# Running the last projection's eight row tiles inside attention

## The chip, the cores and the metric

The kernel runs on one core of one Trainium2 chip. The metric is device time in microseconds (us), the median of several runs. In the profile PE is TensorE, DVE is VectorE, ACT is ScalarE, POOL is GpSimd and SP is SyncE, which here issues every DMA.

## The reference

1024 rows x of 512 numbers are layer-normed. Two branches start from the normed rows xn: attention, and a feed-forward network with quantised weights, whose output goes through a SiLU and gates attention's output.

```python
xn = layernorm(x)
q = rmsnorm(heads(xn @ Wq.T)) ; k = rmsnorm(heads(xn @ Wk.T)) ; v = heads(xn @ Wv.T)   # 32 query heads, 8 key heads, 128 wide
scores = q @ k.T / sqrt(128) + slope[head] * (key - query)                             # causal
s = softmax(scores) @ v ; s = rows(s) @ Wo.T
g = silu(ffn(xn))
out = x + s * g
```

## The kernel before

Float32 products are made of three float16 products each (`mm3`, L151 to L153: high x high, high x low, low x high), added up in PSUM. Almost all PE work in this part is on these three lines, and it is told apart by its tiles.

The feed-forward network runs first, and its gates go to a scratch tensor `gd`. Then come twelve **projections**, numbered k = 0 to 11: for each pair of key heads one `kv` projection and two `q` projections of four heads. So k = 9 is the last `kv`, and k = 10 and 11 are the queries of groups 6 and 7. A projection has eight **row tiles** of 128 rows (`Projection.tile`): twelve products of 128x512 with the normed rows `xth`/`xtl` as weights and the projection's split weights `wh`/`wl` moving, into one PSUM slot of the ring "m" (even rows) or "o" (odd rows). ACT reads the slot (a copy into `f`, L660, and squares for the norm, L662; for `kv` also the values). Both rings have two slots, and attention uses them too: "o" for probabilities times values, "m" for the output projection.

After four tiles the half is queued (`queue_half`): the norms are inverted (L687), by a Sqrt on ACT and Newton steps on POOL (L707 to L710) where `by_root` holds, which is k < 10, and else by an integer seed on DVE (L130, L131) and Newton steps alone. Each tile is then normalised on POOL (`normalize`, L716) and split into two halves on DVE (`halves`, L729 and L730). Most pairs are transposed by DMA and stored (L752, L757, L759). Projection 10's are stored as they are (L735) and transposed when loaded, and projection 11's stay in SBUF until `last_queries` transposes them (L974). `prepare` splits the weights of the next projection meanwhile, on ACT (L631) and DVE (L633), and squares those of the one after (L570).

**Attention** goes in steps. A step n is one query tile of 128 rows of one head; there are 256, in blocks of eight: a group g of four heads and a block qb of 256 queries, in the order of `FIRST_ORDER`, `ORDER` and `LAST_ORDER` (within group 4: queries 2, 3, 0, 1, steps 128 to 159). PE's order in a step is written out by hand: the scores of step n, then the products of step n - 9 with the values (`values`), with a part of the output projection ahead of the last of them. The others follow at lags: DVE adds the position term and finds the maximum (`biased`, L1041) one step later, ACT takes exponentials (L1047) in the same step, ACT makes the high half (L1066) three steps later and DVE the low half (L1074) four steps later; then SP transposes both by DMA (L1082, or L1077 for queries 0) into `pT`, which is a slot of the ring "pT" or "wide". The output projection's weights are loaded (L991), scaled on POOL (L994) and split on ACT (L1000) and POOL (L1001). Sums of the output projection over the groups are kept in `y` rows (L1147, L1149), which lie in `xth`/`xtl`, since the last tile is done by then.

The first eight steps are hosted by projections 10 and 11: `project_all` calls `early_tile` after each of their 16 row tiles, which advances attention by half a step. A branch on the keys' lengths stands just before projection 10; the profiled execution takes the side where far keys of the steep heads are skipped.

The clock that `finishing` uses counts one per row tile, then one per step. So `TILES + 24` is step 32: the last projection's halves are inverted at steps 32 and 44 (`LAST_ROOTS`), and its pairs split at steps 54, 86, 118, 150, 182, 229, 232 and 237 (`LAST_PAIRS`, rows 4, 5, 6, 7, 2, 3, 0, 1).

Of the kernel before, what the change touches and what calls it, by code (L numbers as in the profile page):

```python
# [53 lines left out]
VALUES_STEP = 24  # L54


LAST_ROOTS = {1: 24, 0: 36}
LAST_PAIRS = {4: 46, 5: 78, 6: 110, 7: 142, 2: 174, 3: 221, 0: 224, 1: 229}
LAST_QUERIES = {4: 217, 5: 219, 6: 225, 7: 227, 2: 233, 3: 235, 0: 241, 1: 243}

WO_SPLIT = 6
WO_SCALE = 8
WO_LOAD = 10

GATE_LOADS = [211, 219, 235, 251]
GATE_SUMS = [227, 235, 251, 259]
PF_BUFS = 5
P16_BUFS = 5
OH_BUFS = 8
# [40 lines left out]
def attention_gated_by_ffn_kernel(ctx, tc, x, gu_w, gu_z, gu_s, dn_w, dn_z, dn_s, wq, wkv, wo, qnw, knw, out):  # L110
# [440 lines left out]
    class Projection:  # L551
# [97 lines left out]

        def tile(self, t):  # L650
            n, half, r = self.n, t // HT, t % HT
            if r == 0:
                self.f[half] = rings["f"].take(F32, HT, n, HD)
                self.ss[half] = rings["ss"].take(F32, HT, n)
                self.jk = rings["jk"].take(BF16, NH, HD)
            ps = ps1("o" if t % 2 else "m")
            rows = slice(t * P, (t + 1) * P)
            for j in range(KT):
                mm3(ps, (xth[:, j, rows], xtl[:, j, rows]), (self.wh[:, j, :], self.wl[:, j, :]), j == 0, j == KT - 1)
            se.copy(self.f[half][:, r], ps[:, : n * HD].rearrange("p (g d) -> p g d", g=n))  # L660
            for i in range(n):
                se.activation(  # L662
                    self.jk[:, i],
                    ps[:, i * HD : (i + 1) * HD],
                    AF.Square,
                    scale=STEEPER[i] / Q_SCALE if self.kind == "q" else 1.0,
                    accum_out=self.ss[half][:, r, i : i + 1],
                )
            if self.kind == "kv":
                if t == 0:  # L670
                    self.v16 = rings["v16"].take(F16, 2, NT, 2, HD)
                v16 = self.v16[:, :, t]
                vp = ps[:, 256:512].rearrange("p (g d) -> p g d", g=2)
                se.copy(v16[:, :, 0, :], vp)
                defer(1, lambda: ve.tensor_tensor(v16[:, :, 1, :], vp, v16[:, :, 0, :], ALU.subtract))
                if t == NT - 1:
                    defer(3, self.store_values)
# [227 lines left out]
    def pieces(tag, cols):  # L905
        return [slot[:, c : c + cols] for slot in rings[tag].slots for c in range(0, slot.shape[1], cols)]

    wh_pieces = pieces("wh", QB // 2)
    rings["oh"], rings["ol"] = Ring(wh_pieces[:OH_BUFS]), Ring(wh_pieces[OH_BUFS:])
    rings["wor"] = Ring(pieces("wl", DM))  # L910
    free_pieces = pieces("v16", DM // 2) + pieces("sq", DM // 2)
    rings["woh"], rings["wol"] = Ring(free_pieces[:5]), Ring(free_pieces[5:])
    y_halves = [t.rearrange("p k s -> p (k s)").bitcast(F32) for t in (xth, xtl)]

    def y_rows(t):
        return y_halves[t // HT][:, t % HT * DM : (t % HT + 1) * DM]
# [1 line left out]
    def queue_half(p, half):  # L918

        last = p is projections[-1]  # L920

        def due(steps, i, f):
            if last and i is None:
                c = TILES + LAST_ROOTS[half]
            elif last:
                c = TILES + LAST_PAIRS[half * HT + i] - 4
            else:
                c = clock[0] + (i or 0)
            finishing.setdefault(c + steps, []).append(f)

        due(0, None, lambda: p.inverse(half))
        if p.by_root:
            due(1, None, lambda: p.root(half))
            due(2, None, lambda: p.newton(half, True))
        else:
            for i in range(3):
                due((i + 1) // 2, None, lambda i=i: p.newton(half, i == 0))
        later = int(p.by_root)
        for i in range(HT):
            t = half * HT + i  # L940
            due(4 + later, i, lambda t=t: p.halves(t))
            due(2 + later, i, lambda t=t: p.normalize(t))
# [125 lines left out]
    def split_lo(u, qt):  # L1068
        p, h16 = pf.pop((u, qt)), p16.pop((u, qt))
        nk, k0 = p.shape[1], lowest(u, qt)  # L1070
        if qt == 0:
            pT[u] = rings["wide" if u % 4 < 2 else "pT"].take(F16, NT, 2, QB)
        hi, lo, scale = h16[:, :, 0, :], h16[:, :, 1, :], rows16[u][3][:, qt : qt + 1]
        ve.scalar_tensor_tensor(lo, p, scale, hi, ALU.mult, ALU.subtract)  # L1074
        if u in p16:
            if qt == NQT - 1:
                sp.dma_start_transpose(  # L1077
                    pT[u][:, :NQT].rearrange("p t a (i q) -> p (t a i) q", i=NQT),
                    p16.pop(u).rearrange("p t a i k -> p (t a i k)"),
                )  # L1080
            return
        sp.dma_start_transpose(  # L1082
            pT[u][:, k0 : k0 + nk, :, qt * P : qt * P + P].rearrange("p t a q -> p (t a) q"), h16.rearrange("p t a k -> p (t a k)")
        )
# [40 lines left out]

    gates = {}

    def gate_load(qb):
        gx = rings["f"].take(F32, 2, NQT, DM)
        t0 = qb * NQT  # L1130
        sp.dma_start(gx[:, 0], gd[t0 : t0 + NQT].rearrange("t p c -> p t c"))
        sp.dma_start(gx[:, 1], x[t0 * P : (t0 + NQT) * P, :].rearrange("(t p) c -> p t c", p=P))
        gates[qb] = gx

    def gate_partial(qb, i):

# [41 lines left out]
                        n, taken = n + 1, 0  # L1178
        free = n + (taken > 0)
    near = [False]  # L1180
    TILES = NT * len(projections)

    def at(n):

# [18 lines left out]
    def step(n):  # L1203
# [25 lines left out]
        if n < nn + AV_LAG + 1:  # L1229
            for due in acc_at.get(n, ()):  # L1230
                accumulate(*due)
        finish_step()

        def project():
            for due in op_at.get(n, ()):
                out_proj(*due)

        if at(n - AV_LAG):
            values(*at(n - AV_LAG), project)
        else:  # L1240
            project()
        if done is not None and units[done][:2] == final:
# [5 lines left out]
            if hh == NH - 1:  # L1248
                for due in acc_at.get(nn + AV_LAG + 1, ()):
                    accumulate(*due, other=True)  # L1250
                for i in range(NQT):
                    accumulate(g, qb, i)
        if n in GATE_LOADS:
            gate_load(LAST_ORDER[GATE_LOADS.index(n)][0])
        for i in range(NQT):
            if n - i in GATE_SUMS:
                gate_partial(LAST_ORDER[GATE_SUMS.index(n - i)][0], i)
        for lead, act in ((WO_SPLIT, split_wo), (WO_SCALE, scale_wo), (WO_LOAD, load_wo)):
            for g, first in op_first.items():
                if n + lead - first in range(0, 2 * NH, 2):  # L1260
                    act(g, (n + lead - first) // 2)

    last_ps = None

    def project_all(k):
        p = projections[k]
        for t in range(NT):
# [6 lines left out]
                    projections[k + 2].squares(i)  # L1274
            if t == HT:
                p.undo()
                if k == len(projections) - 3:
                    load_keys(0)
                    for qb in blocks[0][1]:
                        load_queries(0, qb)  # L1280
                elif k == len(projections) - 2:
                    load_values(0)
            if (k, t) == (len(projections) - 3, HT + 1):
                wo_squares_sums()

            row = t if k < len(projections) - 1 else (t + HT) % NT
            p.tile(row)
            finish_step()
            if t % HT == HT - 1:
                queue_half(p, row // HT)  # L1290
            c = (k - len(projections) + 2) * NT + t
            if c >= 0:
                for due in q_at.get(c // 2, ()) if c % 2 == 0 else ():
                    load_queries(*due)
# [4 lines left out]

    def attention(only_near):  # L1300
        near[0] = only_near
        for k in range(len(projections) - 2, len(projections)):
            project_all(k)
        for n in range(NT, nn + AV_LAG + 1):
            step(n)
# [16 lines left out]
                c[:] = old  # L1322

    relative(0)
    for k in range(len(projections) - 2):
        project_all(k)
    flag = nc.values_load(bounded[0:1, 0:1], min_val=0, max_val=1, skip_runtime_bounds_check_because="a comparison's result is 0 or 1")
    was = frozen()
# [44 lines left out]
```

## Time and profile before

| what | value |
|---|---|
| median of 3 runs | 1019.59 us (1016.86 to 1020.25) |
| the profiled execution | 1020.44 us, span 1018.6 us, granted PE clock 0.989 |
| row tiles of projection 9 (first to last L660) | 402.4 to 420.6 us |
| row tiles of projections 10 and 11 | 423.1 to 467.0 us |
| exponentials of steps 8, 16, 24 (L1047) | 469.6, 485.3, 497.4 us |
| exponentials of steps 48, 80, 112, 144, 176, 208 (queries 0 of groups 1 to 6) | 542.9, 605.5, 673.1, 744.8, 813.0, 881.6 us |
| last 8 steps and the end | 981.6 to 1018.6 us |

Times inside the span are counted from its start. A busy PE in the profile is not PE at its peak, since the products' ends are modelled and overlap; the distance between the starts of products is the better measure.

### The profile page before, as it was taken

Reading aid. Unit: us, or ns where it says so; the run is one execution under the profiler, and the core shown is the slowest. Engines: PE = TensorE matmul, PEld = TensorE weight load, DVE = VectorE, ACT = ScalarE, POOL = GpSimd, SP = SyncE. Lnnn points to the kernel's source line nnn. Section 1 sums busy time; section 2 is a strip of 40 time slices with the busy share of each in tenths; the row PEclk is TensorE's granted clock in tenths of the full one; section 3 lists DMA queues with packets and bytes.
Section 4 is the critical chain, followed back from the end, with each engine's and each line's share of the span. In section 5 each row is a group of like instructions: output and inputs, shape, how many; then the busy total and the mean of one; then the engine's idle time right before and its main releaser. Section 6 shows DMA issues by size and latency. Waiting matters only on the chain. (4 is left out here: it accounts for less than half of the span.)

```text
span 1018.6 us, 17980 instructions
## 1 busy us (share of the span) xinstructions
PE 964.7 (95%) x5688; PEld 561.8 (55%) x5688; DVE 857.2 (84%) x1764; ACT 775.5 (76%) x2160; POOL 429.4 (42%) x424
## 2 busy tenths in 40 slices
PE   6899999999999999996998999999999999989995
PEld 4344477854444444444555666665676666656562
DVE  7888998728888878877898998987989989969985
ACT  5777745778878887787887987987879978858861
POOL 2588764216666555564235151051241421530722
PEclk9999999999999999999999999999999999999999
DMA  7132359535998999998898999997999999999994
GB/s 251 37 121 93 104 170 310 187 125 163 204 273 190 245 229 215 236 237 202 172 196 161 206 216 183 227 203 158 231 202 191 212 201 190 202 219 198 218 201 108
DMA packets 425063, 195.74 MB, mean 192 GB/s; under 512 B 371522, under 2 KB 382078, under 8 KB 424958
## 3 DMA queue, kind: packets, MB, share of 16 engines
q1 hardware_dynamic: 424958, 194.50, 85.5%
q8 instruction: 46, 0.75, 0.3%
q14 instruction: 59, 0.48, 0.1%
HBM read 76.27 MB, written 27.27 MB: 102 GB/s over the span
## 5 line engine op out<-in xcount | busy, mean ns | idle before, releaser
L1074 DVE SCALAR_TENSOR_TENSOR p<-pf,row,p 128x384 f16<-128x384 f32 (+7 forms) x256 | 208.8, 816 | 20.9 <-ACT p L1066 18.0
L1047 ACT ACTIVATE pf<-pf,row 128x384 f32<-128x384 f32 (+7 forms) x256 | 184.9, 723 | 41.6 <-DVE row L1041 37.3
L1041 DVE CUSTOM_DVE_ANT_0 pf<-s,trel,cs 128x384 f32<-128x384 f32 (+7 forms) x256 | 191.4, 748 | 19.8 <-PE s L153 19.7
L1066 ACT ACTIVATE p<-pf,row 128x384 f16<-128x384 f32 (+7 forms) x256 | 184.0, 719 | 6.3 <-DMA pT<-p 1.4
L151 PE MATMUL s<-kT,qT 128*128 128x512 f16 (+3 forms) x356 | 115.3, 324 | 11.8 <-DVE row L1041 11.5
L994 POOL TENSOR_SCALAR wl<-wl,rvs 128x512 f32<-128x512 f32 x32 | 53.7, 1677 | 149.0 <-DMA wl<-in_wo 130.0
L152 PE MATMUL s<-kT,qT 128*128 128x512 f16 (+3 forms) x356 | 115.4, 324 | 0.0
L153 PE MATMUL s<-kT,qT 128*128 128x512 f16 (+3 forms) x356 | 114.0, 325 | 0.0
L716 POOL TENSOR_TENSOR f<-f,inv 128x512 f32<-128x512 f32 (+1 forms) x96 | 102.1, 1084 | 1.4
L151 PE MATMUL m<-v,wh 128*128 128x512 f16 x248 | 95.0, 383 | 0.0
L153 PE MATMUL m<-v,wh 128*128 128x512 f16 x248 | 94.9, 383 | 0.0
L151 PE MATMUL o<-pT,vT 128*128 128x256 f16 (+1 forms) x302 | 79.6, 264 | 13.9 <-DMA pT<-p 13.7
L151 PEld LDWEIGHTS <-vT 128*128 128x128 f16 x594 | 58.9, 99 | 57.8 <-DMA pT<-p 15.1
L1110 ACT ACTIVATE wh<-o 128x256 f16<-128x256 f32 x128 | 47.7, 373 | 54.4 <-PE o L153 53.8
L152 PEld LDWEIGHTS <-vT 128*128 128x128 f16 x594 | 58.9, 99 | 41.4 <-issue 4.5
L152 PE MATMUL o<-pT,vT 128*128 128x256 f16 (+1 forms) x302 | 79.6, 264 | 0.0
L153 PE MATMUL o<-pT,vT 128*128 128x256 f16 (+1 forms) x302 | 79.3, 264 | 0.0
L151 PE MATMUL o<-wide,vT 128*128 128x256 f16 (+1 forms) x292 | 75.9, 260 | 3.1 <-DMA wide<-p 3.1
L152 PE MATMUL o<-wide,vT 128*128 128x256 f16 (+1 forms) x292 | 75.9, 260 | 0.0
L153 PE MATMUL o<-wide,vT 128*128 128x256 f16 (+1 forms) x292 | 75.7, 260 | 0.0
L151 PE MATMUL m<-wh,xth 128*128 128x512 f16 x192 | 72.8, 379 | 1.2 <-ACT h L869 1.2
L153 PE MATMUL m<-wh,xtl 128*128 128x512 f16 x192 | 72.8, 379 | 0.0
(200 smaller groups left out, 2531.4 us busy)
## 6 DMA issues: line engine op xcount, KB each, us to landing
qd<-tr SPq DMA_DIRECT2D x48, 256.0 KB, 3.3
qT<-qd SPq DMA_DIRECT2D x24, 512.0 KB, 4.4
wide<-in_wq SPq DMA_DIRECT2D x32, 256.0 KB, 3.7
wo_sq<-in_wo SPq DMA_DIRECT2D x8, 1024.0 KB, 7.8
wl<-in_wo SPq DMA_DIRECT2D x32, 256.0 KB, 3.6
gui<-in_gu_w SPq DMA_DIRECT2D x13, 512.0 KB, 3.7
wide<-in_wkv SPq DMA_DIRECT2D x16, 256.0 KB, 3.8
vd<-v SPq DMA_DIRECT2D x8, 512.0 KB, 4.7
```

The costliest lines, as they stand in the source:

```text
L151: te.matmul(ps, lhsT=lh, rhs=rh, start=first, stop=False)
L152: te.matmul(ps, lhsT=lh, rhs=rl, start=False, stop=False)
L153: te.matmul(ps, lhsT=ll, rhs=rh, start=False, stop=last)
L716: ge.tensor_tensor(f, f, ib, ALU.mult)
L994: ge.tensor_scalar(wor[g, i], wor[g, i], rvs[:, g : g + 1], None, ALU.mult)
L1041: ve.tensor_tensor_reduce(p, ps, trel[g][:, S - w :], cs[:, hh : hh + 1], 3e38, ALU.add, ALU.min, least[:, c])
L1047: se.activation(p, p, AF.Exp, bias=least[:, c], scale=-1.0, accum_out=total[:, c])
L1066: se.activation(p16[u, qt][:, :, 0, :], pf[u, qt], AF.Copy, scale=scale[:, qt : qt + 1])
L1074: ve.scalar_tensor_tensor(lo, p, scale, hi, ALU.mult, ALU.subtract)
L1110: se.activation(oh, av_ps[u], AF.Copy, scale=1.0 / P_SCALE)
```

## The change

Projection 11 is no longer hosted ahead of attention. Projections 9 and 10 host the first eight steps, and the branch stands before projection 9. Each of projection 11's eight row tiles is issued within a step of attention (`LAST_TILES`: step 50 row 4, 53 row 5, 84 row 6, 119 row 7, 150 row 2, 182 row 3, 212 row 0, 215 row 1), behind the step's scores and ahead of its products with the values.

Since projection 11's weights and the normed rows are needed until step 215, buffers are given out otherwise: heads and Wo use the other projection's half of `wh` and `wl` and the ring "tr"; `y` lies in two slots of "f"; gates are loaded into the other two and into `xth`/`xtl`, each in four DMAs of a quarter at steps of their own instead of two DMAs; the first two of every four units use "pT" and the others "wide", the reverse of before. The half norms of projection 11 are inverted at steps 121 and 216, and its pairs split at steps 125, 150, 156, 184, 220, 229, 232 and 237. `by_root` is as it was.

```diff
-LAST_ROOTS = {1: 24, 0: 36}
-LAST_PAIRS = {4: 46, 5: 78, 6: 110, 7: 142, 2: 174, 3: 221, 0: 224, 1: 229}
+LAST_TILES = {50: 4, 53: 5, 84: 6, 119: 7, 150: 2, 182: 3, 212: 0, 215: 1}
+LAST_ROOTS = {1: 121, 0: 216}
+LAST_PAIRS = {4: 125, 5: 150, 6: 156, 7: 184, 2: 220, 3: 229, 0: 232, 1: 237}
 LAST_QUERIES = {4: 217, 5: 219, 6: 225, 7: 227, 2: 233, 3: 235, 0: 241, 1: 243}
...
-GATE_LOADS = [211, 219, 235, 251]
-GATE_SUMS = [227, 235, 251, 259]
+GATE_LOADS = {2: [186, 188, 190, 205], 3: [217, 218, 220, 222], 1: [225, 226, 228, 230], 0: [242, 244, 246, 248]}
+GATE_SUMS = {2: 227, 3: 235, 1: 251, 0: 259}
...
-    wh_pieces = pieces("wh", QB // 2)
-    rings["oh"], rings["ol"] = Ring(wh_pieces[:OH_BUFS]), Ring(wh_pieces[OH_BUFS:])
-    rings["wor"] = Ring(pieces("wl", DM))
+    LAST = len(projections) - 1
+    own = LAST % 2
+    head_pieces = pieces("wh", QB // 2)[(1 - own) * 8 : (2 - own) * 8] + pieces("tr", QB // 2)[8:]
+    rings["oh"], rings["ol"] = Ring(head_pieces[:OH_BUFS]), Ring(head_pieces[OH_BUFS : 2 * OH_BUFS])
+    rings["wor"] = Ring(pieces("wl", DM)[(1 - own) * 2 : (2 - own) * 2] + rings["tr"].slots[:2])
...
-    y_halves = [t.rearrange("p k s -> p (k s)").bitcast(F32) for t in (xth, xtl)]
+    y_halves = rings["f"].slots[:2]
+    x_halves = [t.rearrange("p k s -> p (k s)").bitcast(F32) for t in (xth, xtl)]
...
         def due(steps, i, f):
-            if last and i is None:
-                c = TILES + LAST_ROOTS[half]
-            elif last:
-                c = TILES + LAST_PAIRS[half * HT + i] - 4
+            if last and i is not None:
+                c = step_clock(LAST_PAIRS[half * HT + i]) - 4
             else:
                 c = clock[0] + (i or 0)
...
-            pT[u] = rings["wide" if u % 4 < 2 else "pT"].take(F16, NT, 2, QB)
+            pT[u] = rings["pT" if u % 4 < 2 else "wide"].take(F16, NT, 2, QB)
...
-    def gate_load(qb):
-        gx = rings["f"].take(F32, 2, NQT, DM)
-        t0 = qb * NQT
-        sp.dma_start(gx[:, 0], gd[t0 : t0 + NQT].rearrange("t p c -> p t c"))
-        sp.dma_start(gx[:, 1], x[t0 * P : (t0 + NQT) * P, :].rearrange("(t p) c -> p t c", p=P))
-        gates[qb] = gx
+    def gate_load(qb, i):
+        if i == 0:
+            homes = rings["f"].slots[2], *x_halves, rings["f"].slots[3]
+            gates[qb] = homes[LAST_ORDER.index((qb,))].rearrange("p (a t c) -> p a t c", a=2, t=NQT)
+        t = qb * NQT + i // 2
+        sp.dma_start(gates[qb][:, i % 2, i // 2], x[t * P : (t + 1) * P, :] if i % 2 else gd[t])
...
+    HOSTS = range(LAST - 2, LAST)
+
+    def step_clock(n):
+        return NT * LAST + n - NT
...
         finish_step()
+        for half, due in LAST_ROOTS.items():
+            if n == due:
+                queue_half(projections[LAST], half)
...
+        if n in LAST_TILES:
+            last_tile(LAST_TILES[n])
         if at(n - AV_LAG):
             values(*at(n - AV_LAG), project)
...
-            row = t if k < len(projections) - 1 else (t + HT) % NT
-            p.tile(row)
+            p.tile(t)
...
-        for k in range(len(projections) - 2, len(projections)):
+        for k in HOSTS:
             project_all(k)
...
-    for k in range(len(projections) - 2):
+    for k in range(HOSTS[0]):
         project_all(k)
```

## The prediction

> **What bounds the kernel now.** I read the busy totals first, then busy time by stretches cut where projections and attention blocks begin, then TensorE's own timeline where it stands idle, then ScalarE and VectorE rows for what moves.
>
> ```profile
> PE 964.7 (95%) x5688; PEld 561.8 (55%) x5688; DVE 857.2 (84%) x1764; ACT 775.5 (76%) x2160; POOL 429.4 (42%) x424
> ```
>
> TensorE is busy almost throughout, but the average hides the places where it waits. One row tile costs what lies between the first products of two consecutive tiles:
>
> ```profile
> 304.24 0.38 PE L151 MATMUL m<-wh,xth 128*128 128x512 f16 x1
> ...
> 306.83 0.38 PE L151 MATMUL o<-wh,xth 128*128 128x512 f16 x1
> ```
>
> That is 2.59 us for twelve products (0.216 us apart; the 0.38 overlaps its neighbours). In the stretches below the columns are length, then busy us (and instructions) of PE, weight loads, DVE, ACT and POOL, then granted clock, DMA share and GB/s.
>
> ```profile
> 402.40:423.10 20.70, 20.70 (x98) 9.45 (x97) 18.27 (x39) 14.64 (x63) 12.70 (x18) 1.00 1.13 251
> 423.10:445.50 22.40, 22.40 (x112) 10.56 (x110) 18.43 (x55) 19.21 (x87) 11.70 (x23) 1.00 1.05 253
> 445.50:467.00 21.50, 20.41 (x100) 9.60 (x98) 16.26 (x33) 15.61 (x77) 12.12 (x18) 1.00 0.76 191
> 467.00:485.30 18.30, 11.43 (x78) 7.64 (x78) 11.40 (x37) 14.96 (x49) 7.69 (x6) 0.85 0.88 194
> 673.10:693.30 20.20, 18.17 (x136) 12.77 (x134) 13.49 (x37) 10.71 (x34) 7.14 (x8) 0.92 0.94 184
> 744.80:761.50 16.70, 16.40 (x134) 12.05 (x133) 13.52 (x37) 10.63 (x34) 7.08 (x8) 1.00 1.06 198
> 761.50:774.10 12.60, 12.60 (x81) 7.12 (x80) 12.04 (x34) 11.74 (x33) 1.49 (x1) 1.00 0.85 176
> 774.10:790.80 16.70, 16.70 (x119) 10.45 (x117) 16.49 (x35) 15.25 (x33) 1.58 (x1) 1.00 1.03 206
> 881.60:905.50 23.90, 18.39 (x136) 12.68 (x134) 13.40 (x35) 10.75 (x35) 9.09 (x10) 0.93 1.08 213
> ```
>
> Rows 1 to 3 are projections 9, 10 and 11: PE is full, so each lasts eight tiles plus the scores that it hosts. Row 4 is the start of attention (steps 8 to 15): PE idles 7 us and nothing else is full, so it is a chain of latencies. Rows 6 to 8 are three undisturbed blocks of eight steps (group 4 queries 0 and 1, group 5 queries 2): PE is full in all three, but DVE has 3.2 us free in the first, 0.6 in the second and 0.2 in the third. Rows 5 and 9 are two more blocks of queries 0 (groups 3 and 6), 3.5 and 7.2 us longer than row 6 for the same work. Why is on PE's timeline; the bracket is the idle time and its releaser:
>
> ```profile
> 543.91 0.27 PE L151 MATMUL s<-kT,qT 128*128 128x256 f16 x1 [2.54 <-DVE row L1041]
> 612.27 0.27 PE L151 MATMUL s<-kT,qT 128*128 128x256 f16 x1 [0.75 <-DVE row L1041]
> 686.90 0.28 PE L151 MATMUL o<-pT,vT 128*128 128x256 f16 x1 [2.03 <-DMA pT<-p]
> 756.82 0.28 PE L151 MATMUL o<-pT,vT 128*128 128x256 f16 x1 [0.30 <-DMA pT<-p]
> 825.46 0.27 PE L151 MATMUL o<-pT,vT 128*128 128x256 f16 x1 [0.71 <-DMA pT<-p]
> 890.94 0.28 PE L151 MATMUL o<-pT,vT 128*128 128x256 f16 x1 [1.81 <-DMA pT<-p]
> 899.07 0.28 PE L151 MATMUL o<-pT,vT 128*128 128x256 f16 x1 [3.70 <-DMA pT<-p]
> ```
>
> The first two are ahead of the scores of steps 50 and 84. The other five stand between a step's scores and its products with the values, waiting for transposed probabilities, at steps 119, 151, 183, 212 and 215 (a step's time is read off the exponential of the step before, L1047). The new tiles stand in the same place of steps 119, 212 and 215, and one step earlier at 150 and 182.
>
> **The change, part by part** (against the profiled execution, 1020.44 us, 0.85 above the median of the three runs).
>
> (1) Projection 11's eight tiles leave the front. The eight hosted half-steps move one projection earlier, so their scores cost PE the same; 8 x 2.59 = 20.7 us of full PE go: **-20.7**.
>
> (2) Projection 9 now hosts exponentials, but still takes its roots with Sqrt, as only projections 10 and 11 avoid it. In program order ACT gets four more table loads (to Sqrt and back, twice: two in projection 9, two in 10).
>
> ```profile
> 430.35 1.28 ACT L1047 ACT_TABLE_LOAD   x1
> 431.65 0.51 ACT L1047 ACTIVATE pf<-pf,row 128x256 f32<-128x256 f32 x1
> ```
>
> One load is 1.28 us, and the next activation starts 0.02 us behind it, so four are 5.1 us. Projection 9's ACT: 14.64 + 3 exponentials and 2 scalings of 0.5 to 0.6 (2.7) + three loads (3.8) = 21.1 of 22.3 us. Projection 10's: 19.21 less one load, three exponentials and two scalings (3.9), plus four of each at 0.62 (4.9) and two loads (2.6) = 22.8 of 22.6. DVE in projection 9: 18.27 + 2.7 = 21.0 of 22.3. ACT is on average just full. In the tiles with a load to Sqrt or back it needs 3.8 to 4.6 us (load 1.3, reads 1.1 to 1.5, one or two squarings or a split of 0.65 to 0.74, an exponential or a scaling) against PE's 2.8, while PE's two accumulators allow about 1.3 us of lag. Behind the delayed reads waits PE's tile after next. The lag adds up to some 4.5 us: 4.5 - 1.3 = **+3** (bounds 0 and +5).
>
> The Trainium skill (ScalarE: Activation LUTs, "What ACT_TABLE_LOAD costs") speaks against this part: it counts a drain of about 1.38 us beside each load, some 2.66 us a switch. The row above shows no such gap. By the page four switches are an estimated 10.6 us and part (2) would be about +8, the total about 1016 to 1017.
>
> (3) Steps 8 to 15 take over what projection 11's first tiles hid: four normalisings on POOL (1.04 each where undisturbed), four splits on DVE, half of the stores of the pairs, and transposes and stores of projection 9 that SP is late with. A split is 0.42 + 0.69 = 1.1 us undisturbed; these means include disturbed ones:
>
> ```profile
> L729 DVE CAST a<-f 128x512 f16<-128x512 f32 x64 | 31.0, 484 | 6.8 <-POOL f L716 3.4 <-DMA tr<-a 3.4
> L730 DVE TENSOR_TENSOR a<-f,a 128x512 f16<-128x512 f32 x64 | 51.5, 804 | 2.2
> ```
>
> DVE gets 4.4 us more on 11.40 of 18.3 and still fits. SP does not so easily: between 446 and 467 us it issues some 17 us of transposes (1.2 to 1.3 each) and copies (about 0.55), which must now fit into a projection 9 where SP is already nearly full, or spill here, where some 4 us are free. Four normalisings stand among the scalings of Wo on POOL, which wait for loads through the same SP queue; DVE waits behind them. I take **+4**, between 0 (the latencies hide it) and +8 (12 us spill into 4 free).
>
> (4) The tiles inside attention, 2.59 us each, less the wait that each fills and the slow clock behind it (row 5: 0.08 x 20.2 = 1.6 us lost; row 9: 0.07 x 23.9 = 1.7; around 544, 0.13 of 13.3 = 1.7):
> - Steps 50 and 53: 5.2 - 2.5 - 1.7 = +1.0. The wait is ahead of scores, so the tile doesn't fill it; but its chain runs through POOL's Newton steps and Wo work from 531 to 540, and the Newton steps now stand at steps 121 and 216. Without them the block before, which idles 2 us, should save 1 more: 0.
> - Step 84: 2.6 - 0.75 = +1.8. Step 119: 2.6 - 2.0 - 1.6 = -1.0. Step 150: 2.6 - 0.3 = +2.3. Step 182: 2.6 - 0.7 = +1.9. Steps 212 and 215: 5.2 - 1.8 - 3.7 - 1.7 = -2.0.
>
> Sum **+3.0**, bounds -2 (more small waits fill) and +20.7 (none fills). ACT reads each tile in about 1.5 us; these blocks leave ACT 6 us idle (row 6). PE's products with the values are queued behind each tile; their accumulator is freed by DVE during it in most steps, and at 182, 84 and 212 one step later, under 1 us.
>
> On the slow clock, the Trainium skill (TensorE: Matmul & The Clock Gate, "What's actually happening") asks for an idle window of about 3.4 us. Here waits of 2.03 and 2.54 us already were followed by the slow clock reckoned above. By the page's figure only the wait of 3.70 would bring a credit, and the estimate would be some 3.3 us (1.6 + 1.7) higher.
>
> (5) Splits of four pairs move from blocks of queries 0, where DVE has 3.2 us free, to steps 125, 156, 184 and 220, in blocks of queries 1 where DVE has 0.6. Each adds 1.1 us: 0.5 to 1.1 late, taken as 0.7 since queries 2 behind it have nothing to give: **+2.8** (bounds 0, +4.4).
>
> (6) Gates come in sixteen DMAs of 0.5 us on SP instead of eight, earlier, between other issues. At the end POOL waits 4.15 us for one gate load; that wait should go, but the end hangs on DVE and PE. **0** (bounds -2, +2). Other buffers (pT before wide, y in f) cost nothing: what they hold is dead by then, and the waits that guard them end earlier.
>
> Sum: -20.7 + 3 + 4 + 3.0 + 2.8 + 0 = -7.9; on 1020.44 that is 1012.5, and 0.85 less at the median: 1011.7, rounded to **1011**.
>
> **Rivals.**
> - *Better:* the front absorbs everything and the splits hide: -20.7 + 1 + 0 + 1 + 0 = -18.7, about 1001. For it: row 4 has idle time on every engine. Against it: ACT at 101%.
> - *The front is the bound:* parts (2), (3) and (5) at their upper ends, 5 + 8 + 4.4, and (4) at +3: -0.3, about 1019. For it: SP and ACT are full before and after.
> - *Slower, the waits only move:* transposed probabilities come from SP's queue behind DVE, and DVE waits for PE's scores. If a tile delays the scores of the next steps and so the later transposes as well, the wait returns a few steps on and PE pays all of 20.7: -20.7 + 3 + 4 + 20.7 + 2.8 = +9.8, about 1029. It makes the kernel slower once less than 6.7 of the forecast's fill of 17.7 us (20.7 - 3.0) is real. Against it: the values lag scores by nine steps, so the transpose awaited was issued from scores long before the tile, and DMA goes on during the tile.
>
> **How the numbers follow.** Forecast 0.58 (1004 to 1016), better 0.14, front-bound 0.12, waits move 0.16. A difference of 0.3% (3 us) is about what a measurement of this kernel can tell from none. Faster: 0.58 + 0.14 + 0.03 = 0.75; same: 0.07 + 0.01 = 0.08; slower: 0.02 + 0.15 = 0.17. The range 1001 to 1021 leaves out the slower rival and a little of the better one.
>
> **What would show it.** Right: attention's step 8 starts 16 to 20 us earlier; step 16 about 14; the waits for pT ahead of products with the values at steps 119, 212 and 215 are gone or under 0.5 us, and the clock there is 1.00; blocks (4, 0) and (5, 0) are about 2 us longer; blocks (g, 1) with a split about 0.7 longer; ACT shows four table loads amid the projections, and L660 there waits less for PE. Wrong: PE idle in projections 9 and 10 above 5 us, steps 8 to 15 above 24 us, or a wait for pT in the steps just after each tile.

## The result and the profile after

The changed kernel takes 1028.37 us (median of 10 runs, 1026.27 to 1032.14) against 1019.95 for the kernel before on the same chip (10 runs, 1016.86 to 1026.79): a ratio of 1.0079, 95% interval 1.0057 to 1.0100. It is slower, where the forecast had 1011. The profiled execution took 1032.14 us (span 1030.3), 3.8 above the median.

The busy totals say little: the same work, spread over 11.7 us more.

```profile
PE 967.7 (94%) x5688; PEld 563.4 (55%) x5688; DVE 862.5 (84%) x1764; ACT 781.1 (76%) x2164; POOL 426.5 (41%) x424
```

Busy time by stretches of the changed kernel (columns as before: length, then busy PE, weight loads, DVE, ACT, POOL, then granted clock, DMA share, GB/s):

```profile
402.40:423.10 20.70, 19.33 (x96) 8.98 (x94) 17.05 (x42) 13.52 (x56) 11.04 (x14) 1.00 1.08 247
423.10:445.50 22.40, 18.04 (x87) 8.23 (x86) 16.57 (x46) 22.16 (x81) 9.87 (x15) 1.00 1.13 292
445.50:459.60 14.10, 8.19 (x44) 4.04 (x42) 12.48 (x33) 11.32 (x53) 9.41 (x19) 0.93 0.75 148
459.60:483.70 24.10, 15.01 (x72) 9.10 (x72) 22.87 (x46) 12.62 (x36) 17.16 (x22) 0.57 0.85 228
...
692.20:707.30 15.10, 13.44 (x85) 7.52 (x84) 13.61 (x39) 11.87 (x33) 5.88 (x14) 1.00 0.61 131
...
888.80:914.70 25.90, 22.88 (x157) 15.00 (x156) 11.63 (x35) 13.87 (x53) 6.25 (x7) 0.93 1.06 191
914.70:932.40 17.70, 14.86 (x84) 7.92 (x83) 16.40 (x39) 11.89 (x34) 12.24 (x19) 0.90 0.76 156
```

Rows 1 to 3 are projections 9 and 10 with the hosted steps: PE, full or nearly so before, now idles 1.4, 4.4 and 5.9 us. Row 4 is steps 8 to 15: 24.1 us instead of 15.7, with DVE busy for 22.9 of it and PE on a slow clock. Rows 5 and 7 are the blocks of group 3 and group 6, queries 1, which took 12.60 and 13.25 before; row 6 is group 6, queries 0, 23.86 before.

TensorE's timeline of the changed kernel, longest waits (idle time and releaser in brackets):

```profile
427.98 0.38 PE L153 MATMUL m<-wl,xth 128*128 128x512 f16 x1 [2.80 <-DVE wl L634]
...
456.18 0.27 PE L152 MATMUL s<-kT,qT 128*128 128x256 f16 x1 [3.33 <-DVE row L1043]
459.57 0.48 PE L152 MATMUL s<-kT,qT 128*128 128x384 f16 x1 [2.58 <-DVE row L1043]
...
702.29 0.38 PE L152 MATMUL s<-kT,qT 128*128 128x512 f16 x1 [1.66 <-DVE row L1043]
...
894.66 0.37 PE L152 MATMUL o<-pT,vT 128*128 128x256 f16 x1 [3.02 <-DMA pT<-p]
...
924.46 0.32 PE L152 MATMUL s<-kT,qT 128*128 128x384 f16 x1 [2.61 <-DVE row L1043]
```

The waits for transposed probabilities at steps 119 and 151 are gone. Those of steps 212 and 215 have become one of 3.02 at step 210, ahead of both tiles. New waits stand in the front and where roots and splits now are (702, 924); these are for DVE. The chain of waits says the same; its DMA share was 4% before, all of it `pT<-p`:

```profile
PE 36%; DVE 6%; issue 3%; ACT 2%; DMA 2%; POOL 1%; DVEq 0%
```

Below I use the start of a block of eight steps (the exponential of its first step) and its length. The account of the two profiled executions is:

| stretch, us | before | after | difference | forecast |
|---|---|---|---|---|
| start of step 8 | 469.6 | 459.6 | -10.0 | -17.7 |
| steps 8 to 15 | 15.7 | 24.1 | +8.4 | +4 |
| steps 16 to 247 | 496.3 | 510.7 | +14.4 | +5.8 |
| step 248 to the end | 37.0 | 35.9 | -1.1 | 0 |

Five profiled executions (after, and four of the experiments below) run the same front. In them step 16 starts between 478.1 and 483.7 (mean 481.1), so a single one moves by some 3 us either way, while steps 8 to 15 take 23.2 to 24.1 in all five. From step 32 on most blocks repeat within 0.3 us where nothing in them differs; block (6,0) (group 6, queries 0) does not: it takes 22.6 to 25.9 us in the six executions that run the changed kernel's own code there (the changed kernel, and the runs without Sqrt, splits or keys, with all four at once, and with pairs in queries 0).

### The profile page after: what moved, and what is told of

Read it like the earlier page. It is cut to its first block, busy times and chain, and to the rows that moved or that the text cites. A ratio compares the mean times of both kernels' runs of the same rounds, so it can differ in the third digit from the quotient of the medians.

```text
span 1030.3 us, 17983 instructions
## 1 busy us (share of the span) xinstructions
PE 967.7 (94%) x5688; PEld 563.4 (55%) x5688; DVE 862.5 (84%) x1764; ACT 781.1 (76%) x2164; POOL 426.5 (41%) x424
## 4 chain that ended last, share of the span: by engine, by line
PE 36%; DVE 6%; issue 3%; ACT 2%; DMA 2%; POOL 1%; DVEq 0%
PE o L152 4%; PE o L153 4%; PE o L154 4%; PE s L152 4%; PE s L154 4%; PE s L153 4%; PE m L152 4%; PE m L154 4%; PE m L153 4%; DVE pf L1043 2%; DVE p L1076 2%; DMA pT<-p 1%; ACT p L1068 1%; ACT pf L1049 1%; DVE tr L1117 1%
## 5 line engine op out<-in xcount | busy, mean ns | idle before, releaser
L152 PE MATMUL s<-kT,qT 128*128 128x512 f16 (+3 forms) x356 | 115.7, 325 | 25.3 <-DVE row L1043 24.6
L152 PE MATMUL m<-v,wh 128*128 128x512 f16 x248 | 94.8, 382 | 0.3 <-DVE f L1149 0.3
L154 PE MATMUL m<-v,tr 128*128 128x512 f16 x248 | 94.5, 381 | 0.0
L996 POOL TENSOR_SCALAR wl<-wl,rvs 128x512 f32<-128x512 f32 x16 | 26.3, 1641 | 143.6 <-DMA wl<-in_wo 124.6
L152 PE MATMUL o<-wide,vT 128*128 128x256 f16 (+1 forms) x302 | 79.4, 263 | 3.3 <-DMA wide<-p 2.6
L1117 DVE SCALAR_TENSOR_TENSOR tr<-o,wh 128x256 f16<-128x256 f32 x128 | 53.5, 418 | 34.1 <-ACT wh L1112 33.2
L152 PE MATMUL o<-pT,vT 128*128 128x256 f16 (+1 forms) x292 | 76.6, 263 | 4.4 <-DMA pT<-p 4.4
L153 PE MATMUL o<-wide,vT 128*128 128x256 f16 (+1 forms) x302 | 79.4, 263 | 0.0
L154 PE MATMUL o<-wide,vT 128*128 128x256 f16 (+1 forms) x302 | 79.1, 263 | 0.0
L153 PE MATMUL o<-pT,vT 128*128 128x256 f16 (+1 forms) x292 | 76.5, 262 | 0.0
L154 PE MATMUL o<-pT,vT 128*128 128x256 f16 (+1 forms) x292 | 76.3, 262 | 0.0
L731 DVE TENSOR_TENSOR a<-f,a 128x512 f16<-128x512 f32 (+1 forms) x96 | 73.0, 760 | 3.3
L153 PE MATMUL m<-wl,xth 128*128 128x512 f16 x192 | 72.8, 379 | 2.8 <-DVE wl L634 2.8
```

Of the source, the lines that this page charges most:

```text
L152: te.matmul(ps, lhsT=lh, rhs=rh, start=first, stop=False)
L153: te.matmul(ps, lhsT=lh, rhs=rl, start=False, stop=False)
L154: te.matmul(ps, lhsT=ll, rhs=rh, start=False, stop=last)
L731: ve.tensor_tensor(lo, f, hi, ALU.subtract)
L996: ge.tensor_scalar(wor[g, i], wor[g, i], rvs[:, g : g + 1], None, ALU.mult)
L1117: ve.scalar_tensor_tensor(ol, av_ps.pop(u), 1.0 / P_SCALE, oh, ALU.mult, ALU.subtract)
```

## Experiments: the front

**No Sqrt in projection 9.**

```diff
-            self.by_root = k < 3 * HKV // 2 - 2
+            self.by_root = k < 3 * HKV // 2 - 3
```

> Projection 9 takes its half norms by seed and Newton steps, as 10 and 11 do, so the four extra table loads of ACT go. Theory 'the front is late' (the eight tiles that left the front saved almost nothing there: step 16 starts at 483.7 us against 485.3 before; ACT's table loads and late weights, then eight splits on DVE took it back): ACT loses 4 x 1.28 = 5.1 us of work and DVE no longer waits 3.6 us for a root; step 8 starts 2 to 5 us earlier, total -3 (-1 to -5). Rival 'the waits only move' (the tiles inside attention are paid in full, the front is as forecast): nothing in the front was lost to ACT, total within 1 us.

Measured: 1027.10 us, ratio to before 1.0079 (1.0051 to 1.0107), no different from the changed kernel. Step 16 starts at 481.3, inside the spread of unchanged fronts. The table loads are in the trace, but taking them out alone gives nothing that can be told from none.

**No splits of projection 10** (its eight pairs are neither normalised nor split; what lies in another slot is stored in their place):

```diff
+            if self.k == len(projections) - 2:
+                return
...
+                defer(1, lambda: sp.dma_start(qd[self.i][t], rings["tr"].slots[4].bitcast(F16)))
+                return
```

> Leaves out the normalising (POOL) and splitting (DVE) of projection 10's eight pairs; their stores stay, from another buffer, so group 6 computes with other queries. Theory 'the front is late': eight splits of 1.1 us or more and eight normalisings land in steps 8 to 15, where DVE was busy 22.9 of 24.1 us; without them these steps take 15 to 17 us, total -7 (-5 to -11). Rival 'the waits only move': steps 8 to 15 are a chain of latencies through SP and lose 1 to 2 us.

Measured: 1028.38 us, ratio 1.0099 (1.0075 to 1.0123). Steps 8 to 15 still take 24.1 us without these splits. The expectation missed; VectorE's timeline of this run shows what took their place:

```profile
463.81 0.42 DVE L1122 SCALAR_TENSOR_TENSOR tr<-o,wh 128x256 f16<-128x256 f32 x1 [5.84 <-DMA kd<-tr]
```

This is the low half of a head (`heads_lo`), which now lies in a slot of "tr". The slot still holds projection 9's keys on their way to memory, so DVE stands for 5.84 us, and PE for 5.33 behind it.

**No keys of projection 9** (not transposed, not stored; groups 6 and 7 read the keys of 4 and 5):

```diff
+            if self.k == len(projections) - 3:
+                return
...
-        sp.dma_start(kT[g].rearrange("p t a k -> p t (a k)"), kd[g // 2][:, g % 2])
+        sp.dma_start(kT[g].rearrange("p t a k -> p t (a k)"), kd[min(g // 2, HKV // 2 - 2)][:, g % 2])
```

> Leaves out the transposes and stores of projection 9's keys (groups 6 and 7 read the keys of groups 4 and 5 instead), so SP loses eight transposes of about 1.24 us and eight copies of about 0.55 us, 14.3 us in all; nothing else changes. Theory (the front is bound by SP's queue, and DVE's wait for a slot of tr that is still being stored hangs on it): step 16 starts 6 to 12 us earlier than in the changed kernel's 483.7, and the whole is 6 to 10 us shorter. Rival (VectorE with eight splits and ScalarE with its table loads bind steps 8 to 15 just as much): 3 us or less, steps 8 to 15 still over 22 us.

Measured: 1030.19 us, ratio 1.0085 (1.0052 to 1.0119); step 16 at 479.6, steps 8 to 15 22.1 us. The theory of SP's queue as the one bound falls; the rival fits.

**All of these at once**, and the heads' low halves and Wo in each other's slots of "tr":

```diff
-    ... + pieces("tr", QB // 2)[8:]
+    ... + pieces("tr", QB // 2)[:8]
...
-    ... + rings["tr"].slots[:2])
+    ... + rings["tr"].slots[2:4])
```

> Takes away every cost of the front that the traces name, at once: no Sqrt in projection 9; projection 10's pairs neither normalised nor split (left out, whatever lies in the slot is stored); projection 9's keys neither transposed nor stored (left out); and heads' low halves in tr slots 0 and 1, Wo in slots 2 and 3. Theory (these four are the front's costs): step 16 starts near 470 (467 to 474), 12 to 16 us earlier than in the changed kernel, as the forecast had it with its -13.7 against before, and the whole is 11 to 16 us shorter. Rival (the scores, exponentials and products of steps 8 to 15 are themselves a chain that needs some 20 us there): step 16 not ahead of 477, the whole at most 7 us shorter.

Measured: step 16 starts at 469.5, 11.6 us ahead of the mean of the unchanged fronts, and steps 8 to 15 take as long as before the change. The stretches of this run:

```profile
454.20:469.50 15.30, 10.72 (x76) 7.21 (x76) 11.17 (x34) 12.42 (x37) 10.62 (x17) 0.88 0.91 240
```

DVE's 22.87 us have become 11.17. The whole is 1020.96 us, ratio 1.0005 (0.9989 to 1.0022): 7.4 us less than the changed kernel by the medians, less than the 11 to 16 expected, and 12.9 less by the spans (the changed kernel's profiled execution lies 3.8 above its median, this run's 1.7 below). So the four together are the front's loss in steps 8 to 15, while each of the three taken out alone leaves the others to take its place. Pairs and triples of them, and the exchange of slots alone, were not run; how the loss divides among them stays open.

## Experiments: the tiles and the splits in attention

**Pairs split in blocks of queries 0 again:**

```diff
-LAST_ROOTS = {1: 121, 0: 216}
-LAST_PAIRS = {4: 125, 5: 150, 6: 156, 7: 184, 2: 220, 3: 229, 0: 232, 1: 237}
+LAST_ROOTS = {1: 144, 0: 216}
+LAST_PAIRS = {4: 149, 5: 151, 6: 179, 7: 183, 2: 220, 3: 229, 0: 232, 1: 237}
```

> The half norms of rows 4 to 7 of projection 11 are inverted at step 144 instead of 121, and their pairs split at steps 149, 151, 179 and 183 instead of 125, 150, 156 and 184: all in blocks of queries 0. Theory that Newton steps, normalising and splits cost time only where DVE has none to give: block (3, 1) goes from 15.2 back to 12.6, (4, 1) from 13.4 to 12.6, blocks (4, 0) and (5, 0) stay within 0.5; total -3 (-1.5 to -4). Rival that these blocks are longer because waits moved there from the tiles: they stay as long, total within 1 us.

Measured: 1028.22 us, ratio 1.0109 (1.0083 to 1.0136): nothing gained. Block (3,1) (group 3, queries 1) falls to 12.6 and (4,1) to 12.6 as expected, but (4,0) rises from 19.6 to 20.1 and (5,0) from 19.9 to 21.4. Those blocks had room for splits only while they had no tile.

**The tiles in steps 8 to 15**, roots and pairs at the steps of the kernel before:

```diff
-LAST_TILES = {50: 4, 53: 5, 84: 6, 119: 7, 150: 2, 182: 3, 212: 0, 215: 1}
-LAST_ROOTS = {1: 121, 0: 216}
-LAST_PAIRS = {4: 125, 5: 150, 6: 156, 7: 184, 2: 220, 3: 229, 0: 232, 1: 237}
+LAST_TILES = {8: 4, 9: 5, 10: 6, 11: 7, 12: 2, 13: 3, 14: 0, 15: 1}
+LAST_ROOTS = {1: 32, 0: 44}
+LAST_PAIRS = {4: 54, 5: 86, 6: 118, 7: 150, 2: 182, 3: 229, 0: 232, 1: 237}
```

> The eight tiles at steps 8 to 15, rows 4 to 7 and then 0 to 3, with half norms and pairs at the steps of the kernel before (32 and 44; 54, 86, 118, 150, 182, 229, 232, 237). PE was idle 16 us of these 24.1. Theory 'the front is late' (DVE bounds steps 8 to 15, PE is free there): the tiles cost 0 to 6 us there, and from step 16 on the kernel takes the 533 us of before instead of 547; total -10 (-6 to -13) against the changed kernel. Rival that these steps hang on SP's queue and ACT: ACT's reads of 8 x 1.5 us come on top, steps 8 to 15 take 34 us or more, total -3 or less.

Measured: **1015.05 us, ratio 0.9966 (0.9947 to 0.9985)**, faster than both kernels. With all eight tiles in them, steps 8 to 15 take 26.2 us, 2.1 more than without any in the changed kernel, since PE had idled there (9.1 us of the 24.1 by the row, not the 16 of the expectation; the rest was the slow clock). Steps 24 to 31 grow too, from 11.6 to 13.5, so the tiles cost some 4 us where they now stand. From step 16 to 247 the run takes 494.0 us, 16.8 less than the changed kernel.

**The same tiles, roots and pairs late.** Only `LAST_TILES` is changed from the changed kernel, which divides those 16.8 us.

> The eight tiles one each in steps 8 to 15, but the roots and the pairs' splits left at the changed kernel's steps (121, 216; 125, 150, 156, 184, 220, ...). From step 16 to the end the changed kernel takes 546.6 us, the run with both moved forward 529.8. Theory (about half of these 16.8 us is the moved splits and Newton steps, in the blocks of steps 120, 152 and 216, the other half the tiles): 536 to 540 from step 16 on, with block (3,1) at 15.1, (6,1) at 17 to 18, and blocks (1,0), (2,0), (3,0), (4,0) and (5,0) as in the run with both moved; total 1020 to 1025. Rival (the tiles cost it all): within 2 us of the run with both moved, (3,1) at 12.6 and (6,1) at 13.2.

Measured: 1020.70 us, ratio 1.0004 (0.9984 to 1.0024). Steps 16 to 247 take 499.5: **5.5 us of the 16.8 are the late roots and pairs, 11.2 the tiles** (13.1 from step 32 on, less the 1.9 of steps 24 to 31). The late ones cost +2.5 in (3,1), +1.2 in (4,0), +0.8 in (4,1) and +4.5 in (6,1), and give back 2.7 in (1,3), where the Newton steps were. Block (6,1) in the run with early pairs, and in this one:

```profile
902.30:915.60 13.30, 13.30 (x85) 7.59 (x84) 12.68 (x34) 11.86 (x34) 3.93 (x3) 1.00 0.89 195
```

```profile
901.50:919.20 17.70, 14.51 (x84) 7.72 (x83) 16.39 (x39) 11.88 (x33) 12.24 (x19) 0.90 0.78 156
```

DVE has five instructions more, a split of 1.1 us undisturbed and three on 16 columns for the root, but its busy time grows by 3.7 us: POOL now does Newton steps, normalisings and gate sums there (12.24 us instead of 3.93). VectorE's split in the changed kernel's (6,1), undisturbed 0.42 and 0.69:

```profile
920.95 1.25 DVE L730 CAST a<-f 128x512 f16<-128x512 f32 x1 [0.93 <-POOL f L717]
922.24 1.63 DVE L731 TENSOR_TENSOR a<-f,a 128x512 f16<-128x512 f32 x1
```

POOL is busy without a gap from 919.7 to 929.2.

**Three products per tile** instead of twelve:

```diff
-            for j in range(KT):
-                mm3(ps, ..., j == 0, j == KT - 1)
+            kt = 1 if self.k == len(projections) - 1 else KT
+            for j in range(kt):
+                mm3(ps, ..., j == 0, j == kt - 1)
```

> Each of projection 11's eight tiles takes three products instead of twelve (nine of twelve are left out); everything else of the tile stays. TensorE has 8 x 9 x 0.216 = 15.6 us less. Theory (some of each tile does fill a wait, and the blocks with moved splits are held by VectorE): 7 to 8 us shorter than the changed kernel (5 to 11). Rival (waits only move, and the tiles are paid in full): 14 to 16 us shorter. Rival (the tiles are hidden and only the reads and splits cost): 0 to 3.

Measured: 1024.49 us, ratio 1.0041 (1.0022 to 1.0061), 3.9 less than the changed kernel by the medians and 5.3 less in steps 16 to 247. 15.6 us of PE bring back a third or less: by the medians between the first theory (5 to 11) and the second rival (0 to 3), by the steps at the theory's lower edge.

**Short reads:**

```diff
+            if self.k == len(projections) - 1:
+                se.copy(self.f[half][:, r, :, :4], ps[:, : n * 4].rearrange("p (g d) -> p g d", g=n))
+                se.activation(self.ss[half][:, r], ps[:, :n], AF.Copy, scale=0.0, bias=1.0e8)
+                return
```

> The twelve products of each of the eight tiles stay, and ScalarE's reading is cut: a copy of 4 of every 128 columns instead of 0.59 us, and one short instruction in the place of four squares with sums (about 1.0 us); projection 11's queries are left out that way. Some 1.2 us of 1.63 per tile go from ScalarE, 9.6 us in all. Theory (the tile costs by what queues behind its reads on ScalarE, since taking out nine of twelve products gave only 4 us): 5 to 9 us shorter than the changed kernel. Rival (the reads lie beside TensorE's work and cost nothing as long as the products are there): 0 to 3.

Measured: 1027.69 us, ratio 1.0076 (1.0047 to 1.0106): nothing that the times show. Steps 16 to 247 are 2.1 us shorter, which is no more than block (6,0) gives (23.4 against 25.9), and that lies inside this block's spread. Taken alone the reads look free, as the rival had it.

**Both:**

> Both: three products per tile (nine of twelve left out) and the short reads. Next to nothing of a tile is left but its place in TensorE's order and its PSUM slot. Theory (products and reads are two ways around the same time, so that each alone gains little and both together gain nearly all of the tiles' share): 9 to 12 us shorter than the changed kernel, with blocks (1,0), (2,0) and (3,0) within 0.7 us of the run with the tiles in steps 8 to 15. Rival (the slot that a tile holds and its place in the order are the cost): at most 6 us shorter, the three blocks still over 1 us longer.

Measured: 1021.73 us, ratio 1.0019 (0.9999 to 1.0040), 6.6 us less by the medians. Steps 16 to 247 take 498.3, 12.4 less than the changed kernel and more than 5.3 + 2.1; without block (6,0) it is 9.3 against 4.2 and nothing. By the blocks:

| block with a tile, us | tiles in steps 8 to 15, late pairs | changed | three products | short reads | both |
|---|---|---|---|---|---|
| (1,0), two | 13.35 | 17.11 | 16.85 | 17.12 | 15.29 |
| (2,0) | 16.00 | 17.64 | 17.45 | 17.63 | 16.06 |
| (3,0) | 17.45 | 18.91 | 18.67 | 18.91 | 17.09 |
| (4,0) | 17.55 | 19.61 | 17.28 | 18.91 | 17.78 |
| (5,0) | 17.01 | 19.88 | 17.87 | 20.06 | 18.37 |
| (6,0), two | 25.34 | 25.87 | 24.71 | 23.44 | 22.75 |

In (2,0) and (3,0) either half of the tile costs what the whole costs, and without both the cost is gone. In (4,0) and (5,0) it is the products: (4,0) took 18.9 to 19.8 where nothing in it differed, so its 18.91 with short reads is no gain. In (6,0) the spread of 22.6 to 25.9 hides what a tile costs. The expectation held for (2,0) and (3,0) and missed (1,0), still 1.9 above. It also missed by the medians (9 to 12 expected): the spans differ by 10.4, but the changed kernel's profiled execution lies 3.8 above its median. Even so the last block (step 248 to the end) took 39.7 us here, 3.8 more than in the changed kernel; why is left open. Block (2,0) without most products, with short reads, and with both:

```profile
602.30:619.70 17.40, 15.97 (x131) 11.45 (x130) 12.29 (x35) 12.07 (x43) 5.32 (x7) 1.00 0.98 197
```

```profile
599.40:617.00 17.60, 17.60 (x140) 12.27 (x139) 12.40 (x35) 10.81 (x36) 5.27 (x7) 1.00 0.93 195
```

```profile
600.10:616.20 16.10, 16.00 (x132) 11.44 (x130) 12.28 (x35) 10.77 (x36) 5.32 (x7) 1.00 1.04 214
```

With the products PE is full (17.60 of 17.60). Without them PE has 1.4 us to spare and the block is hardly shorter; the timeline of the run with three products shows why:

```profile
611.46 0.40 ACT L1113 ACTIVATE wh<-o 128x256 f16<-128x256 f32 x1
...
611.89 0.42 DVE L1118 SCALAR_TENSOR_TENSOR tr<-o,wh 128x256 f16<-128x256 f32 x1 [1.29 <-ACT wh L1113]
...
613.06 0.74 DVE L1152 SCALAR_TENSOR_TENSOR f<-m,isg,f 128x512 f32<-128x512 f32 x1
...
613.86 0.38 PE L152 MATMUL m<-v,wh 128*128 128x512 f16 x1 [1.33 <-DVE f L1152]
```

ACT reads the tile from 609.98 to 611.5. The high half of a head stands behind that on ACT; DVE waits for it, and behind DVE's wait stands the sum that frees the "m" slot PE needs. With the products in place the same waits of ACT and DVE are in the trace, and PE is at work meanwhile.

**The run with tiles in steps 8 to 15, without Sqrt in projection 9 and with the slots of "tr" exchanged** (the two diffs above):

> The eight tiles one each in steps 8 to 15 with roots and splits at the steps of the kernel before (as in the run with the tiles in steps 8 to 15), and also no Sqrt in projection 9, and heads' low halves in tr slots 0 and 1, Wo in slots 2 and 3. Theory (waits of the front are what is left to take): 3 to 6 us less than the run with the tiles in steps 8 to 15 alone, 1009 to 1012. Rival (with the tiles there TensorE is full again and covers these waits): within 2 us of it.

Measured: 1016.25 us, ratio 0.9959 (0.9937 to 0.9981); step 16 at 484.0 against 483.8. The rival was right: where PE is full the waits of the front are covered.

**The run with tiles in steps 8 to 15, roots at idle steps of POOL:**

```diff
-LAST_ROOTS = {1: 32, 0: 44}
+LAST_ROOTS = {1: 22, 0: 27}
```

> The eight tiles one each in steps 8 to 15, pairs split at the steps of the kernel before, but the half norms inverted at steps 22 and 27 instead of 32 and 44, where POOL is idle but for short fills of zeros (488 to 509 us in the run with roots at 32 and 44). Theory (POOL's twelve Newton steps among the scalings of Wo delay the block of steps 40 to 47: 19.30 us there with them, 16.54 with the roots at 121 and 216): that block falls to 16.5 to 17, the whole 2 to 4 us below that run, 1011 to 1013, some 0.7% under the kernel before. Rival (POOL's late Wo work, not the Newton steps, sets that block, or the wait returns in the next): within 1 us of that run, 1014 to 1016.

Measured: **1013.91 us (12 runs, 1007.15 to 1019.72), ratio 0.9944 (0.9921 to 0.9968)**, the lowest median of all. The block of steps 40 to 47 falls from 19.3 to 16.6 as the theory had it. The medians differ by 1.1 and the intervals overlap, so the gain over the roots at 32 and 44 is shown for that block alone; for the whole it is not shown, and the spans (1010.4 against 1013.6) are one execution each.

## Why the prediction was wrong

**(1)** -20.7 stands: from 402.4 us to step 8, PE's busy time fell from 65.15 to 45.53 us, 19.6, and the slow clock at the end of that stretch hides about one more. **(2), the first step that failed, in size: +10.7 in the profiled execution instead of +3** (+5.3 to +10.7 in the five with this front, step 8 at 454.1 to 459.6; all above its bound of +5). The four extra table loads are there, each 1.28 us. But the step counted engine totals and not what is queued behind them. In ScalarE's and VectorE's timeline of the changed kernel:

```profile
423.03 0.63 ACT L571 ACTIVATE sq<-wide 128x512 bf16<-128x512 f32 x1 [4.50 <-DMA wide<-in_wq]
...
425.18 0.38 ACT L675 CAST v<-o 128x256 f16<-128x256 f32 x1
425.57 1.28 ACT L702 ACT_TABLE_LOAD   x1
426.87 0.21 ACT L702 ACTIVATE inv<-ms 128x8 f32<-128x8 f32 x1
427.11 0.20 DVE L707 RECIPROCAL inv<-inv 128x8 f32<-128x8 f32 x1 [3.61 <-ACT inv L702]
427.23 0.70 DVE L634 SCALAR_TENSOR_TENSOR wl<-wide,am,wh 128x512 f16<-128x512 f32 x1
```

ACT waits 4.50 us for the weights of projection 11, which SP issued between 410.2 and 418.3, amid the transposes (401.5 to 410.1 before the change). The table load and the root stand behind that wait, DVE behind the root, the split of projection 10's weights behind DVE, and PE's 2.80 at 427.98 is the end of it. PE is idle 12 us in projections 9 and 10, over the 5 named as a sign of error. In the execution with short reads ACT's wait is 0.62 and PE's 2.80 is missing, and with pairs in queries 0 they are 2.74 and 1.03; these two start step 16 earliest of the five.

This chain is read from the traces; no run shows it to be the whole cause. Without the Sqrt (no root to wait for) PE's wait is gone from there, but one of 4.00 behind DVE stands at 437.77, and step 8 starts at 456.9, amid the five. With short reads (where the chain is missing) and with all four costs of the front taken out, step 8 starts at 454.1 and 454.2, still over 5 us later than -20.7 alone would put it. What holds these 5 us stays open.

The Trainium skill (ScalarE: Activation LUTs, "What ACT_TABLE_LOAD costs"), which the prediction weighed, counts a drain of about 1.38 us beside a load. These rows have none: the cast ends at 425.56, the load runs from 425.57, and the root starts 0.02 us after it.

**(3), +8.4 instead of +4** (+7.5 to +8.4 in the five), at or over its upper bound of +8. The term counted four splits; the trace has seven in steps 8 to 15 and one just ahead, since all of projection 10's pairs come late, and three of them took 2.0 to 2.8 us while POOL was busy. And (6) said of other buffers that what they hold is dead by then: the slots of "tr" were not, as the 5.84 us showed. The sign named ("steps 8 to 15 above 24 us") came true by a hair: 24.1.

**(4), the step that decides: the tiles cost 11.2 us, not 3.0** (about 9.5 if block (6,0) is taken by the means below). The prices by step were fair where a tile met no wait: 84 +1.6 (forecast +1.8), 150 +2.1 (+2.3), 182 +2.9 (+1.9). The credits for filled waits failed at 50, 53 and 119. At 50 and 53 (forecast 0) block (1,0) is 3.8 longer than without tiles; the Newton steps' leaving does give 2.2 in the block before, more than the 1 reckoned, but it comes without tiles as well. At 119 (-1.0) the length against before is right, -1.3, for the wrong reason: the wait is all but gone without a tile, so the tile is paid with +1.5 after all. At 212 and 215 (-2.0) the profiled execution alone misleads: it is 2.0 longer than before, but the six executions with these tiles take 22.6 to 25.9 us (mean 24.6), and the four with the tiles in steps 8 to 15 take 25.3 to 26.4 (mean 25.9). The tiles do fill the wait at step 215, which is 3.16 to 3.73 us in those four and absent in the six. Here it is in the run with the tiles in steps 8 to 15 and in the one with late pairs:

```profile
895.93 0.28 PE L152 MATMUL o<-wide,vT 128*128 128x256 f16 x1 [3.16 <-DMA wide<-p]
```

```profile
895.09 0.28 PE L152 MATMUL o<-wide,vT 128*128 128x256 f16 x1 [3.56 <-DMA wide<-p]
```

Against the kernel before, a new wait at step 210 or 211 (1.8 to 3.1 us in nine of these ten) takes the fill back. It stands there without tiles as well, so the tiles do not make it; the gate loads and the other pT buffers are in all ten, and which of them does was not tried. And "ACT reads each tile in about 1.5 us; these blocks leave ACT 6 us idle" was the wrong question: ACT's idle time lies elsewhere than behind the tile, as the rows around 611.46 show.

**(5), +5.5 instead of +2.8**, over its bound of 4.4, and that is net of the 2.7 given back in (1,3): the splits were priced undisturbed and without the Newton steps and normalisings that move along.

**The rivals.** "Slower, the waits only move" gave 1029 and the time is 1028.4, but its sum is not what happened: its front was the forecast's, and PE waited less in attention (18.1 us of gaps from step 16 on against 22.3), with the DMA share of the chain halved. By terms, the two profiled executions: -20.7 + 10.7 + 8.4 + 11.2 + 5.5 - 3.5 = +11.6 (the spans differ by 11.7), the last being what steps 16 to 247 take less than before in the run with the tiles in steps 8 to 15 (494.0 against 496.3), and the end (-1.1). The medians differ by 8.4; the changed kernel's profiled execution has the latest front of the five and is 3.8 above its median. "The front is the bound" had the front nearly right (-20.7 + 13 = -7.7; measured -1.6, and -4.2 by the mean of the five) and the tiles too low.

On the clock, the wait of 2.61 at 924 was followed by about half clock for 3.4 us (0.90 over the row). The Trainium skill (TensorE: Matmul & The Clock Gate, "What's actually happening") asks for an idle window of about 3.4 us; this case does not agree, as the prediction had taken it. Nor does the length of one wait decide: 2.54 ahead of step 50 of the kernel before brought the slow clock, while 2.60 at the same place, in the run with the tiles in steps 8 to 15, left it at 1.00. What tells them apart is in the traces. In attention the granted clock drops to 0.50 for whole stretches of 3.41 us, and within one execution these start whole multiples of 3.41 us apart (894.60 and 925.32 in the changed kernel: nine of them). So time can be cut into windows of 3.41 us, and what counts is how long PE idles within one window. The 2.54 lies almost wholly in one (kernel before, two windows that follow each other):

```profile
541.43:544.84 3.41, 0.93 (x8) 0.73 (x8) 1.29 (x4) 2.71 (x9) 2.68 (x3) 1.00 0.79 175
544.84:548.25 3.41, 3.41 (x17) 1.98 (x16) 3.41 (x7) 2.48 (x7) 2.68 (x4) 0.50 0.69 165
```

The 2.60 is parted between two, so that the fuller one has PE busy for 1.55 and idle for 1.86 (run with the tiles in steps 8 to 15):

```profile
538.10:541.51 3.41, 2.67 (x22) 1.71 (x21) 1.55 (x5) 1.09 (x3) 3.41 (x3) 1.00 1.05 218
541.51:544.92 3.41, 1.55 (x12) 1.10 (x12) 1.92 (x5) 3.33 (x9) 2.68 (x3) 1.00 0.98 234
544.92:548.33 3.41, 1.89 (x19) 1.21 (x17) 3.41 (x9) 1.88 (x8) 2.68 (x4) 1.00 0.58 124
```

Counted over steps 16 to 247 of all fourteen profiled executions, among windows at full clock: 29 were followed by a slow one, with PE idle for 2.02 us or more in 28 of them and 1.94 in the other; 1980 were not, and PE idled 1.96 us at most in any of these.

## What to carry to other kernels

A task put into a full stage can be paid in full even where one engine has time for it, because it enters several queues: in two blocks of six a tile's products and its reads were two ways around the same time, so that removing either brought little and both brought all. In two others the products alone were most of the cost. Before work is moved, look for the stage where every engine idles at once and ask whether the work can be put there: eight tiles cost some 4 us in the starting steps of attention and 13 from step 32 on. And one profiled execution can mislead: a block that moves by 3 us from one to the next can't price a tile of 2.6. A change that frees 20 us in a full stage also takes away the cover of all that ran beside it; price that by the instructions that still have to come, in their queues, not by engines' totals.

## What was not expected of the hardware

DVE's splits of 128x512 took 0.42 and 0.69 us alone and up to 1.26 and 1.63 us while POOL was busy (in part of the cases; others stayed at 0.42 and 0.69). And whether a wait of PE brings the slow clock is not told by its length alone: 2.54 and 2.61 us did, 2.60 did not. It went by PE's idle time within one window of 3.41 us: from about 2.0 us on, the next window had half the clock; below, it did not.
